# Dealing out the first six transfers of a block exchange between SyncE and GpSimd

## The chip, the cores and the metric

The kernel runs on one NeuronCore of a Trainium2 chip. The metric is the device time of one execution in microseconds (us), the median of several runs. Engines are called as in the profile: PE is TensorE (matmuls; PEld its weight loads), DVE is VectorE, ACT is ScalarE, POOL is GpSimd, SP is SyncE, which here only issues DMAs.

## What is computed

The reference adds an attention output to its input. With eight batches of 512 tokens, width 512, and 16 heads of 32:

```
Q, K, V = heads(x @ W.T + b) for Wq, Wk, Wv
cQ, cK  = Q + heads(tokens @ Wq.T + bq), K + heads(tokens @ Wk.T + bk)
attn    = softmax(cQ @ cK.T / sqrt(32))
out     = x + merge(attn @ V)
```

Everything is float32; `tokens` is one conditioning row per batch.

## The kernel before

**Groups and windows.** The work is cut into 32 groups t = 4b + g: batch b and one of four groups g of four heads. The main loop (line 1237) runs over t, and nearly all of its turns are calls of `thirds(t)` (line 1131). The stretch of such a turn is called *window* t here, counted from PE's first matmul of `weighted(t-1)` (line 856, L808), the product of group t-1's exponentials with V. A turn also makes the scores of group t+1, the transposed exponentials of group t, and a quarter of the next batch's projections (matmuls L461, by a scheme of seven half-size products whose sums are made on DVE and POOL). The order on PE, ACT, DVE and POOL is that of the program text (`manual_schedule`, line 235); SP's instructions, all DMA issues, are placed by the recording layer. Every engine takes its own list strictly in order.

**Exponentials that are kept.** Row maxima and row sums need the scores with queries on partitions; the product with V needs the exponentials with keys on partitions. For groups 2 to 28 (`KEPT`, line 71) the exponentials of the first two query chunks are made once, in `denominators` (L693), kept in SBUF (`room`, line 209) and turned. Those of the other two chunks are made a second time in the other orientation (`exponentials_of_rest`, L766, L777, L787). The turning has two steps: DVE turns 32x32 blocks in place (`turn_kept`, L660), and then six pairs of 32-partition blocks (a, g), a < g, change places by DMA.

**An exchange.** That second step is `swap_kept(t, move)` (line 665), called an *exchange*. It has three rounds of six DMAs of 128 KB each:

- move 0, the *first round*: block (a, g) is copied to a place aside (`between`)
- move 1, the second round: block (g, a) is copied to (a, g), once that one was copied aside
- move 2, the third round: the copy aside goes to (g, a)

SP issues the first three transfers (n = 0, 1, 2) of the first round and all of the second; POOL issues the other three of the first round (n = 3, 4, 5) and all of the third. The first two rounds of exchange t+1 stand at the end of window t (lines 1184 to 1186); the third round stands in the middle of window t+1 (lines 1155 to 1162), ahead of `split_max` on POOL. PE reads the exchanged blocks in the second half of L808 in `weighted(t+1)`, that is in window t+2.

**POOL's list around the first round.** In every window POOL has, in this order: two sums of the output of the group before (`send`, L881 and L882, which wait for DVE's L880), two or three sums of the projection scheme (L535 to L537 for q and k, L1220 and L1221 for v), the third round (six L674), `split_max` (L707 to L710), `masked` (L833), the residual's bias (L204), further sums of the projections (L1209 or L535 to L537), and then POOL's part of the first round of the next exchange (L674). Where t is a multiple of four (a new batch is prepared), `combine_x` (line 380) adds four sums of x for the next batch's projections: L387 and L388 after L204, and L390 and L391 at the end of the window, directly ahead of the first round of exchange t+1. So the exchanges with t % 4 = 1 follow these sums.

**SP's list.** It holds, per window: four loads of the residual (L191), the first and second round, four stores of a finished group (L885), four loads of x (L173), and one transposing DMA of the row maxima (`turn_max`, L719), which waits for `split_max`.

**What waits for POOL's sums.** In window t with t % 4 = 1 the sums L535 to L537 go into DVE's L551 and L486 (`other_products`, lines 551 to 556), which read two PSUM banks. PE needs these banks again for the second pair of the next scores, L641 (`row_max`).

Of the kernel before, what the change touches and what calls it, by code (L numbers as in the profile page):

```python
# [17 lines left out]
def kernel(  # L18
# [38 lines left out]
    nc = tc.nc  # L57
# [606 lines left out]

    def swap_kept(t, move, last=nc.gpsimd):

        def part(a, g):
            return kept[t][a * BL : (a + 1) * BL, g].rearrange("p c h s -> p (c h s)")

        for n, (a, g) in enumerate(APART):  # L670
            at = (n + 2) % HG * BL
            aside = between[at : at + BL, n // HG].rearrange("p i s -> p (i s)")
            to, of = [(aside, part(a, g)), (part(a, g), part(g, a)), (part(g, a), aside)][move]
            (last if move == 2 or move == 0 and n >= 3 else nc.sync).dma_start(to, of)  # L674

    def denominators(t, qc, w=HG, js=range(HG)):

# [453 lines left out]
    def thirds(t, made):  # L1131
# [16 lines left out]
        for i in (1, 2):  # L1148
# [6 lines left out]
            if i == 1:  # L1155
                if t + 1 in KEPT:
                    swap_kept(t, 2)
                split_max(t + 1)
                if t + 1 in KEPT:
                    turn_max(t + 1)  # L1160
                else:
                    swap_kept(t, 2)
# [17 lines left out]
            if i == 2:  # L1180
                if r == 0:
                    combine_x(b + 1, 1, nc.gpsimd)
                load_residual(t + 1)
                if t + 1 in KEPT:
                    for move in range(2):
                        swap_kept(t + 1, move)
            else:
                bias_residual(t)
                if r == 0:
                    combine_x(b + 1, 0, nc.gpsimd)  # L1190
# [104 lines left out]
    def latest_pair(of, among):  # L1295
        pairs = [(j, j + 1) for j in of if j + 1 in of and among & {j, j + 1}]
        return max(pairs, key=lambda p: order.index(p[0]) + order.index(p[1]))

    last = latest_pair(order, {order[7]})
# [59 lines left out]
    t = T - 3  # L1359
# [20 lines left out]
    t = T - 2  # L1380
# [27 lines left out]
    t = T - 1  # L1408
# [103 lines left out]
```

## Time and profile before

| | |
|---|---|
| median of 3 runs | 666.72 us (666.71 to 668.23) |
| the profiled execution | 667.76 us |
| its span, first to last instruction | 666.0 us |
| granted TensorE clock, mean | 0.996 |
| busy PE / DVE / ACT / POOL | 98% / 89% / 81% / 64% of the span |
| DMAs of L674 | 243 issued by SP, 243 by POOL |

The span is one profiled execution; 1.76 us of its time lie outside the span. A busy PE holds waits between matmuls too, since the ends of matmuls are modelled; so it is better to compare how long equal stretches of work take than to read its busy share. In a timeline row stand the start in us, the time taken in us, the engine, the line, the operation, the tiles, the number of merged instructions, and in brackets the idle time before them and what ended it. Windows of the same parity do equal work on PE.

### The profile page before, as it was taken

Reading aid. Unit: us, or ns where it says so; the run is one execution under the profiler, and the core shown is the slowest. Engines: PE = TensorE matmul, PEld = TensorE weight load, DVE = VectorE, ACT = ScalarE, POOL = GpSimd, SP = SyncE. Lnnn points to the kernel's source line nnn. Section 1 sums busy time; section 2 is a strip of 40 time slices with the busy share of each in tenths; the row PEclk is TensorE's granted clock in tenths of the full one; section 3 lists DMA queues with packets and bytes.
Section 4 is the critical chain, followed back from the end, with each engine's and each line's share of the span. In section 5 each row is a group of like instructions: output and inputs, shape, how many; then the busy total and the mean of one; then the engine's idle time right before and its main releaser. Section 6 shows DMA issues by size and latency. Waiting matters only on the chain.

```text
span 666.0 us, 24768 instructions
## 1 busy us (share of the span) xinstructions
PE 652.7 (98%) x9812; PEld 349.4 (52%) x9812; DVE 589.9 (89%) x821; ACT 542.0 (81%) x1378; POOL 423.6 (64%) x668
## 2 busy tenths in 40 slices
PE   9999999999999999999999999999999999999993
PEld 7345445555555555555555555555555555555421
DVE  3698899999999999998999999999999989995793
ACT  2479988889888888988888898888889888887771
POOL 3541345787666876659757696667875597576531
PEclk9999999999999999999999999999999999999998
DMA  6633157778777787877897787779877757786111
GB/s 178 105 51 63 31 122 161 163 165 187 173 152 174 161 190 154 189 156 167 171 190 167 169 191 172 160 150 170 196 165 176 169 133 175 149 181 138 18 18 32
DMA packets 246183, 97.14 MB, mean 146 GB/s; under 512 B 228842, under 2 KB 229354, under 8 KB 246068
## 3 DMA queue, kind: packets, MB, share of 16 engines
q1 hardware_dynamic: 232644, 62.65, 49.3%
q0 software_dynamic: 11664, 31.87, 17.3%
q8 instruction: 77, 1.26, 0.9%
q10 hardware_dynamic: 1760, 1.05, 0.5%
q14 instruction: 38, 0.31, 0.1%
HBM read 19.75 MB, written 8.39 MB: 42 GB/s over the span
## 4 chain that ended last, share of the span: by engine, by line
PE 95%; DMA 2%; SPq 1%; DVE 1%; issue 0%; DVEq 0%
PE psum L461 43%; PE psum L641 19%; PE psum L808 15%; PE psum L777 7%; PE psum L792 3%; PE psum L766 3%; PE psum L748 2%; SPq L270 1%; PE psum L404 1%; DMA w_q<-in_L_cond_Wq_dram 1%; PE psum L745 1%; PE psum L1336 1%; PE psum L818 1%; DMA store<-in_x_dram 1%; DMA w_k<-in_L_cond_Wk_dram 0%; PE psum L843 0%
## 5 line engine op out<-in xcount | busy, mean ns | idle before, releaser
L693 ACT ACTIVATE psum<-psum,nmax 128x512 f32<-128x512 f32 x263 | 174.8, 670 | 5.0 <-DVE nmax L589 3.9
L589 DVE TENSOR_REDUCE nmax<-psum 128x1 f32<-128x512 f32 x219 | 140.5, 678 | 22.2 <-PE psum L641 19.6
L693 ACT ACTIVATE store<-psum,nmax 128x512 f32<-128x512 f32 x190 | 130.3, 700 | 33.3 <-DVE nmax L589 23.8
L650 DVE TENSOR_REDUCE nmax<-psum 128x2 f32<-128x1024 f32 x127 | 153.7, 1211 | 1.3 <-PE psum L641 1.3
L674 POOL DMA_DIRECT2D store<-store x243 | 121.7, 504 | 48.1 <-DMA store<-store 36.2
L641 PE MATMUL psum<-kT,qT 32*128 32x512 f32 x1024 | 146.7, 616 | 0.0
L787 ACT ACTIVATE store<-psum 128x512 f32<-128x512 f32 x216 | 111.5, 603 | 22.6 <-PE psum L777 22.6
L660 DVE STREAM_TRANSPOSE store<-store 128x1024 f32<-128x1024 f32 x108 | 129.5, 1217 | 0.0
L808 PE MATMUL psum<-store,v 128*32 128x256 f32 x1728 | 99.3, 381 | 0.0
L808 PEld LDWEIGHTS psum<-store,v 128*32 128x32 f32 x1728 | 53.2, 110 | 54.1 <-ACT wT_q L628 19.7
L641 PEld LDWEIGHTS psum<-kT,qT 32*128 32x128 f32 x1024 | 57.8, 183 | 37.3 <-issue 20.2
L881 POOL TENSOR_TENSOR res<-res,recs 128x512 f32<-128x512 f32 x30 | 31.4, 1047 | 69.0 <-DVE res L880 68.9
L693 ACT ACTIVATION_READ_ACCUMULATOR psum<-psum,nmax 128x1 f32 x263 | 56.3, 214 | 0.0
L777 PE MATMUL psum<-qT,kT 32*128 32x256 f32 x864 | 55.8, 373 | 0.0
L461 PE MATMUL psum<-wc_v,xc 128*32 128x256 f32 x768 | 47.7, 379 | 0.0
L204 POOL TENSOR_TENSOR xr<-xr,bvs 128x512 f32<-128x512 f32 x30 | 38.4, 1279 | 12.2 <-DMA x<-in_x_dram 11.4
L461 PE MATMUL psum<-xc,wc_k 128*32 128x256 f32 x720 | 44.5, 379 | 0.0
L461 PE MATMUL psum<-xc,wc_q 128*32 128x256 f32 x720 | 44.5, 379 | 0.0
L777 PEld LDWEIGHTS psum<-qT,kT 32*128 32x128 f32 x864 | 42.3, 184 | 3.4
L693 ACT ACTIVATION_READ_ACCUMULATOR store<-psum,nmax 128x1 f32 x190 | 40.8, 215 | 0.0
L882 POOL TENSOR_TENSOR res<-res,xr 128x512 f32<-128x512 f32 x30 | 38.4, 1279 | 2.4
L758 ACT ACTIVATE store<-psum 128x512 f32<-128x512 f32 x56 | 28.9, 603 | 9.3 <-PE psum L748 7.2
(198 smaller groups left out, 1046.3 us busy)
## 6 DMA issues: line engine op xcount, KB each, us to landing
store<-store SPq DMA_DIRECT2D x243, 128.0 KB, 2.8
store<-store POOLq DMA_DIRECT2D x243, 128.0 KB, 3.7
out_dram<-res SPq DMA_DIRECT2D x122, 64.0 KB, 3.6
xr<-in_x_dram SPq DMA_DIRECT2D x120, 64.0 KB, 3.4
x<-in_x_dram SPq DMA_DIRECT2D x112, 64.0 KB, 3.0
w_q<-in_L_cond_Wq_dram SPq DMA_DIRECT2D x4, 256.0 KB, 5.3
w_v<-in_L_cond_Wv_dram SPq DMA_DIRECT2D x16, 64.0 KB, 2.5
w_k<-in_L_cond_Wk_dram SPq DMA_DIRECT2D x16, 48.0 KB, 3.0
```

Source lines behind the costliest of these rows:

```text
L204: nc.gpsimd.tensor_tensor(xr[t], xr[t], bias, ALU.add)
L461: nc.tensor.matmul(pt[r], still[:, r], moving, start=(kc == kcs[0]), stop=(kc == kcs[-1]))
L589: nc.vector.tensor_reduce(nmax[t][:, qc, j : j + 1, 0], pt, AX.X, ALU.max, negate=True)
L641: nc.tensor.matmul(pt, qkT["q", t][r, qc * P : (qc + 1) * P], qkT["k", t][r, :], start=True, stop=True,)
L650: nc.vector.tensor_reduce(nmax[t][:, qc, pr * 2 : pr * 2 + 2, 0], pt, AX.X, ALU.max, negate=True)
L660: nc.vector.transpose(e, e)
L674: (last if move == 2 or move == 0 and n >= 3 else nc.sync).dma_start(to, of)
L693: nc.scalar.activation(to, of, AF.Exp, bias=nmax[t][:, qc, j, :], accum_out=sums[t][:, qc, j, :],)
L777: nc.tensor.matmul(bank[j][:, i * HS : (i + 1) * HS], qkT["k", t][r, kc * P : (kc + 1) * P], qkT["q", t][r, rest], start=False, stop=(i == 1),
L787: nc.scalar.activation(e[:, i, :], bank[pr * 2 + i], AF.Exp)
L808: nc.tensor.matmul(pt[j * HD : (j + 1) * HD, half * HS : (half + 1) * HS], vs[b % 2][:, kc, (g * HG + j) * HD : (g * HG + j + 1) * HD], e, ...
L882: nc.gpsimd.tensor_tensor(y, y, xr.pop(t), ALU.add)
```

## The change

Of an exchange's first round, SP issues the first transfer and POOL the other five, where it was three and three. In exchanges with t % 4 = 1 SP issues all six and POOL none. The second and third rounds stay as they were. For the 27 exchanges (t = 2 to 28) this makes 21 of the first kind and 6 of the second (5, 9, 13, 17, 21, 25).

```diff
     def swap_kept(t, move, last=nc.gpsimd):
 
+        later = 6 if t % 4 == 1 else 1
+
         def part(a, g):
             return kept[t][a * BL : (a + 1) * BL, g].rearrange("p c h s -> p (c h s)")
 
         for n, (a, g) in enumerate(APART):
...
             to, of = [(aside, part(a, g)), (part(a, g), part(g, a)), (part(g, a), aside)][move]
-            (last if move == 2 or move == 0 and n >= 3 else nc.sync).dma_start(to, of)
+            (last if move == 2 or move == 0 and n >= later else nc.sync).dma_start(to, of)
```

The lists of PE, DVE and ACT are the same in both kernels. On POOL the run of three L674 at the end of a window becomes one of five, or goes. On SP the run of nine L674 becomes one of seven, or of twelve.

## The prediction

> **What bounds the kernel now.** I read the page first: PE is busy nearly all the time.
>
> ```profile
> span 666.0 us, 24768 instructions
> PE   652.7 (98%) x9812; PEld 349.4 (52%) x9812; DVE 589.9 (89%) x821; ACT 542.0 (81%) x1378; POOL 423.6 (64%) x668
> ```
>
> The change leaves PE's work alone, so only time in which PE waits can be won. Since a busy PE hides waits, I cut the main loop into windows, each from PE's first L808 to the next, and took their lengths with the stage view of PE alone. Of the 21 windows that are not in the next table, these are the first two, the last, and the sum:
>
> ```profile
> 110.91:130.08 19.17, 19.17 (x316) 1.00 0.76 169
> 130.08:149.45 19.37, 19.37 (x316) 1.00 0.76 169
> ...
> 575.58:594.75 19.17, 19.17 (x316) 1.00 0.74 163
> sum 405.03, PE 405.03; mean PE 19.29
> ```
>
> Column two is the length in us, then come PE's busy time, the clock and the DMA share. Windows with odd t take 19.15 to 19.18, with even t 19.37 to 19.39, and the sum says the same: 10 x 19.165 + 11 x 19.38 = 404.8. Four windows fall out. Here is one that keeps the time (t = 9, the first row) and the four (t = 13, 17, 21, 25), with the busy time of L641 alone:
>
> ```profile
> 226.55:245.70 19.15, 4.18 (x32) 1.79 (x32) 1.00 0.83 179
> 303.63:323.22 19.59, 4.62 (x33) 2.07 (x32) 1.00 0.78 171
> 381.14:400.78 19.64, 4.67 (x33) 1.87 (x32) 1.00 0.81 177
> 458.69:478.52 19.83, 4.86 (x33) 2.06 (x32) 1.00 0.92 176
> 536.45:556.20 19.75, 4.78 (x33) 2.09 (x32) 1.00 0.71 159
> ```
>
> Against the first row they are 0.44, 0.49, 0.68 and 0.60 us longer, **2.21 us** in all, and L641 is longer by the same 0.44, 0.49, 0.68 and 0.60. So PE loses its time at one place, ahead of the second pair of L641. All four are windows with t % 4 = 1, those in which POOL has just made the last sums of x. The timelines of POOL, of window 9 and then of 13:
>
> ```profile
> 230.77 1.52 POOL L674 DMA_DIRECT2D store<-store  x3
> 232.30 1.06 POOL L881 TENSOR_TENSOR res<-res,recs 128x512 f32<-128x512 f32 x1
> 236.17 0.73 POOL L537 TENSOR_TENSOR qT<-qT 128x256 f32<-128x256 f32 x1
> ```
>
> ```profile
> 308.07 1.30 POOL L391 TENSOR_TENSOR xc<-xT,xc 128x512 f32<-128x512 f32 x1
> 309.29 1.52 POOL L674 DMA_DIRECT2D store<-store  x3
> 310.82 1.06 POOL L881 TENSOR_TENSOR res<-res,recs 128x512 f32<-128x512 f32 x1
> 314.70 0.73 POOL L537 TENSOR_TENSOR qT<-qT 128x256 f32<-128x256 f32 x1
> ```
>
> and of DVE, window 9 and then 13, with the weight load that waits in 13:
>
> ```profile
> 237.64 0.41 DVE L551 TENSOR_TENSOR qT<-psum,qT 128x256 f32<-128x256 f32 x1
> 237.97 1.40 DVE L486 SCALAR_TENSOR_TENSOR qT<-psum,tok,qT 128x512 f32<-128x512 f32 x2
> ```
>
> ```profile
> 308.30 0.65 DVE L880 STREAM_TRANSPOSE res<-psum 128x512 f32<-128x512 f32 x1
> 314.77 0.42 DVE L551 TENSOR_TENSOR qT<-psum,qT 128x256 f32<-128x256 f32 x1
> 315.46 1.41 DVE L486 SCALAR_TENSOR_TENSOR qT<-psum,tok,qT 128x512 f32<-128x512 f32 x2 [0.27 <-POOL qT L537]
> ```
>
> ```profile
> 316.93 0.29 PEld L641 LDWEIGHTS psum<-kT,qT 32*128 32x128 f32 x2 [0.20 <-DVE qT L486]
> ```
>
> In window 13 POOL goes from L391 through three DMA issues into L881 without a pause; L537 ends at 315.43; DVE's L486 waits for it, and PE's L641 for L486, whose reads set its banks free. Counted from the window's start, L486 begins at 315.46 - 303.63 = 11.83 us in window 13 and at 237.97 - 226.55 = 11.42 in window 9. That 0.41 is the 0.44 that PE loses. In window 9 L537 ended at 236.90, 10.35 us into the window, 1.07 before L486 began.
>
> **The change part by part.**
>
> *Exchanges with t % 4 = 1 (six of them).* POOL loses three issues between L391 and L881. They take 1.52 us. What is late next? L881 also needs DVE's L880, which ended at 308.95 in window 13, and L391 ended at 309.37; so POOL, not DVE, sets L881, which starts 310.82 - 309.37 = 1.45 us sooner. L537 then ends 315.43 - 1.45 = 313.98, 10.35 us into the window, as in window 9, and L486 finds it done 1.07 us before its time. The worst of the four is window 21:
>
> ```profile
> 470.00 0.73 POOL L537 TENSOR_TENSOR qT<-qT 128x256 f32<-128x256 f32 x1
> ```
>
> It ends at 470.73, or 12.04 into the window, and would end at 10.59: still 0.83 us early. So all four losses go: **-2.2 us** (2.21 against window 9, 2.17 against the 19.16 of its kind). In windows 5 and 9 nothing waits, so there is nothing to win.
>
> SP gets three issues more there. An issue on SP takes 0.54 us in the middle, so twelve take 6.5 us; the nine of before took 8.24:
>
> ```profile
> L674 SPq DMA_DIRECT2D store<-store x243: 507/541/2282, 91.4 to 604.7; - x122
> L674 POOL DMA_DIRECT2D store<-store x243: 489/489/677, 92.4 to 609.5; - x122
> ```
>
> ```profile
> 307.64 8.24 SPq L674 DMA_DIRECT2D store<-store  x9
> ```
>
> since the second round waited for POOL's late copies. That wait goes, so the stores (L885), the x loads and the transposing DMA behind on SP come at about their old times; I take 0, between -1.7 (8.24 to 6.5) and +1.6 (three issues with no wait saved). Their cover is SP's place off the path: no row of PE above waits for it.
>
> *The other 21 exchanges.* POOL gets two issues more, 0.98 us at 489 ns, ahead of L881; 42 x 0.49 = 20.5 us of POOL's time, less 18 x 0.49 = 8.8 in the six. What hides it is POOL's wait there:
>
> ```profile
> POOL res L881 <- DVE res L880: 68.9, 24, 5.0
> POOL store L674 <- DMA store<-store: 36.2, 29, 2.6
> ```
>
> 24 waits with 2.9 us in the mean. The shortest that I found where three issues came in a row is that of window 14:
>
> ```profile
> 328.64 1.04 POOL L881 TENSOR_TENSOR res<-res,recs 128x512 f32<-128x512 f32 x1 [1.24 <-DVE res L880]
> ```
>
> 1.24 holds 0.98. One other is shorter, in window 16, where POOL's third issue came 2.04 us late:
>
> ```profile
> 365.90 0.49 POOL L674 DMA_DIRECT2D store<-store  x1 [2.04 <-issue]
> 367.18 1.04 POOL L881 TENSOR_TENSOR res<-res,recs 128x512 f32<-128x512 f32 x1 [0.78 <-DVE res L880]
> ```
>
> There L881 could come 0.2 us late, for which I count nothing. Cost 0; without the cover at most 0.98 in a window.
>
> SP loses two issues there (1.1 us), but gains little: its second round begins when the first copy has landed, and that one stays on SP behind the residual's loads.
>
> *The shift d.* What the trace can't show is whether the second round, and with it the third on POOL, now ends later by some d in these 21. Two copies come by way of POOL's queue instead of SP's:
>
> ```profile
> store<-store SPq DMA_DIRECT2D x243, 128.0 KB, 2.8
> store<-store POOLq DMA_DIRECT2D x243, 128.0 KB, 3.7
> ```
>
> ```profile
> DMA to landing us min/median/max: 2.2/3.5/6.1
> ```
>
> So d lies between -1.1 (two SP issues saved) and 6.1 - 2.8 = 3.3 (every copy as slow as the slowest). The medians are 0.9 apart, but the second round runs at one issue in 0.54 us from its start, while POOL issues a first-round copy every 0.49, so copies keep ahead of it. I take d = 0, nearest to the medians, and keep both ends. A d matters in window 13 and its like: POOL's third round in windows 12, 16, 20, 24 runs on into L387 to L391 of the next window, so L537 there is later by d. The stall is then max(0, s + d - 1.45), with s = 0.44, 0.49, 0.68, 0.60. Up to d = 0.77 nothing returns; at 0.9 it is 0.13.
>
> The Trainium skill (SBUF — State Buffer, section "A bandwidth-pool intuition that's wrong (but worth ruling out)") speaks against moving issues to GpSimd: a DMA whose descriptors GpSimd writes, some 620 ns alone, takes some 3100 when VectorE holds their common port in a copy. By that rule, as an estimate, five issues would take up to 15 us instead of 2.5, which is rival 3 below with a d of several us. The row of POOL's L674 above disagrees: the longest of 243 issues took 0.677 us, with DVE busy for 89% of the span.
>
> *Sum.* -2.2 + 0 + 0. Span 666.0 to 663.8; the profiled execution 667.76 to 665.6; that one is 1.04 above the median of 666.72, so the median becomes **664.5 us**.
>
> **The rivals.**
>
> 1. *Part of it comes back.* d between 0.8 and 1.45. At d = 1.2 the four stalls are 0.19, 0.24, 0.43 and 0.35, 1.2 in all: 665.7. For it: POOL's third rounds already wait 36.2 us for landings. Against: the first copy, which starts the second round, does not move.
>
> 2. *Nothing measurable.* L641's wait has another cause that ends at the same time, or d is close to 1.45 to 2: 666.7, between 666 and 667.5. For L486 the trace names POOL's L537, and in window 9 POOL is earlier and PE has no wait; that speaks against another cause.
>
> 3. *Slower.* d passes 1.45 and POOL's lag is larger than before. It decides from there: at d = 3 the four stalls are 1.99, 2.04, 2.23 and 2.15, 8.4 us where 2.2 were, and windows 5 and 9 (s = -1.07) get 0.5 each: +7.2, 673.9. PE's read of the exchanged blocks would tell at about the same d. In a tight exchange, 14:
>
> ```profile
> 336.63 2.48 POOL L674 DMA_DIRECT2D store<-store  x5 [2.20 <-DMA store<-store]
> ```
>
> ```profile
> 342.53 2.80 PE L808 MATMUL psum<-store,v 128*32 128x256 f32 x48
> ```
>
> the last copy's issue begins at 338.62 and the read 1.8 us into L808, at 344.3: 5.7 us later, against landings of 3.7 in the middle and 6.1 at most. What speaks against it is the 0.9 between the medians.
>
> **How the numbers follow.** Forecast 664.5 (664.0 to 665.0): 0.64. Rival 1 (665.0 to 666.2): 0.16. Rival 2 (666.2 to 667.5): 0.09. Rival 3 (668 to 676): 0.11. The range 664.0 to 666.5 takes the first two and a little of rival 2, 0.82. A measurement of this kernel can tell about 0.3%, 2.0 us, from no change, and 2.2 lies just over it: below 664.7 I put 0.46, nearly three quarters of the forecast's chance. Slower by over 0.3% is rival 3 and a little of rival 2, 0.12. The rest, 0.42, is within.
>
> **What would show it.** In the changed kernel's trace the windows 13, 17, 21 and 25 should be 19.15 to 19.2 us long with L641 at 4.2; L881 there should follow L391 at once, and L486 have no wait for L537. The other windows should keep 19.16 and 19.38, with L881 still waiting for L880. SP's twelve issues in window 13 should end by about 316. The prediction is wrong if the third round in windows 12, 16, 20, 24 ends more than 0.8 us later in its window than before, if L881 gets late in one of the 21, or if PE's second half of L808 waits for a landing.

## The result, and the profile after

| | before | after |
|---|---|---|
| median of 9 runs | 666.71 us (665.47 to 668.23) | **661.34 us** (659.82 to 668.35) |
| ratio of the times | | **0.9945** (95%: 0.9919 to 0.9971) |
| the profiled execution | 667.76 us | 665.04 us |

The change gains 5.4 us where 2.2 were forecast: faster, by more than the range allowed. The page of after:

```profile
span 662.8 us, 24720 instructions
PE 651.4 (98%) x9812; PEld 350.7 (53%) x9812; DVE 590.1 (89%) x821; ACT 542.7 (82%) x1378; POOL 435.6 (66%) x692
store<-store POOLq DMA_DIRECT2D x267, 128.0 KB, 3.7
```

POOL issues 267 DMAs instead of 243 and PE does the same work. To see where the time went, I cut each span in three with the stage view of PE: the start, the windows t = 3 to 28 (from PE's first L808, L810 in after, of one to that of the next), and the tail behind the start of window 29. The second and the third, of before and of after (columns as in the prediction):

```profile
110.84:614.56 503.72, 503.72 (x8123) 1.00 0.78 169
614.56:665.97 51.41, 39.96 (x400) 0.94 0.12 22
```

```profile
110.08:616.78 506.70, 502.96 (x8123) 1.00 0.79 168
616.78:662.80 46.02, 39.97 (x400) 0.99 0.13 24
```

The windows, where the prediction saw the whole effect, are 3.0 us *longer* in this execution of after. The **tail is 5.39 us shorter**, and in it PE does the same 39.96 us of work. So the gain comes from a stretch in which the change touches no instruction. The clock column of the tails (0.94 and 0.99) does not explain it: the granted clock is 1.00 from 614.56 to 660.0 in before and from 616.78 to 661.7 in after, and 0.50 from 660.2 and from 661.9 on, where PE has no work left (its last matmul ends at 655.6 and 657.8).

What ends the tail? The instructions of the last line (L1507, L1509 in after) that are no arithmetic, before and then after; the columns are the durations in ns (min/median/max) and the first and last start in us:

```profile
L1507 POOLq DRAIN  x3: 34/102/11361, 653.8 to 665.7; - x3
L1507 SPq DRAIN  x3: 7/7/7, 659.3 to 665.5; - x3
```

```profile
L1509 POOLq DRAIN  x3: 34/102/3434, 656.1 to 662.5; - x3
L1509 SPq DRAIN  x3: 7/7/130, 661.6 to 662.3; - x3
```

and POOL's last sum, before and after:

```profile
653.88 1.28 POOL L1432 TENSOR_TENSOR res<-res,store 128x512 f32<-128x512 f32 x1
```

```profile
656.11 1.27 POOL L1434 TENSOR_TENSOR res<-res,store 128x512 f32<-128x512 f32 x1
```

In before POOL's first DRAIN, in which it waits at the end of its list, takes 11.36 us, to 665.2; that is 10.05 after the last sum ended (its end is 655.15 with the decimals of the trace), and SP, which had waited for its last stores, was done at 659.3. POOL sets the end, alone, for 5.8 us. In after the DRAIN ends 2.13 us after the last sum, at 659.5, and SP's wait at 661.6 comes last. The chain of waits of before doesn't show this DRAIN at all; its line by engine is

```profile
PE 95%; DMA 2%; SPq 1%; DVE 1%; issue 0%; DVEq 0%
```

Now the windows of after. The first row is window 13, the others are 18, 21 and 24:

```profile
302.81:321.98 19.17, 19.17 (x316) 1.00 0.80 168
...
399.10:419.85 20.75, 19.49 (x316) 1.00 0.76 170
...
459.04:479.54 20.50, 19.86 (x315) 1.00 0.84 176
...
518.81:539.18 20.37, 19.49 (x316) 1.00 0.82 181
```

Windows 13, 17 and 25 are clean, as forecast (19.17, 19.19 and 19.16). But windows 18 and 20 to 24 lose time at the second half of L810, which reads the exchanged blocks. In window 18, POOL and then PE:

```profile
399.52 0.49 POOL L676 DMA_DIRECT2D store<-store  x1 [2.63 <-issue]
```

```profile
402.29 1.93 PE L810 MATMUL psum<-store,v 128*32 128x256 f32 x32 [1.26 <-DMA x<-in_x_dram]
```

The last copy of exchange 17's third round is issued at 399.52 and lands at 401.99, and PE goes on at 402.29. The brackets do not name what was waited for, but the semaphore instructions in the trace do. PE's, for this copy, lasts from 399.90 to 402.03. POOL's, ahead of the issue at 399.52, lasts from 396.38 to 399.02, until a copy that SP issued at 393.49 has landed (398.99). So a late exchange holds up PE: this is the second place of the prediction's rival 3.

In window 21 the first place is back too. L641 is 4.67 us long there (4.20 in window 13), and POOL and DVE show why:

```profile
471.08 0.73 POOL L537 TENSOR_TENSOR qT<-qT 128x256 f32<-128x256 f32 x1
```

```profile
471.84 1.41 DVE L486 SCALAR_TENSOR_TENSOR qT<-psum,tok,qT 128x512 f32<-128x512 f32 x2 [0.26 <-POOL qT L537]
```

L537 ends 12.77 us into the window, later than before's 12.04, though no issue stands between L391 and L883 any more.

### The profile page after: what moved, and what is told of

Same layout as the page of the kernel before. It is cut to its first block, busy times and chain, and to the rows that moved or that the text cites. A ratio compares the mean times of both kernels' runs of the same rounds, so it can differ in the third digit from the quotient of the medians.

```text
span 662.8 us, 24720 instructions
## 1 busy us (share of the span) xinstructions
PE 651.4 (98%) x9812; PEld 350.7 (53%) x9812; DVE 590.1 (89%) x821; ACT 542.7 (82%) x1378; POOL 435.6 (66%) x692
## 4 chain that ended last, share of the span: by engine, by line
PE 88%; SPq 4%; DMA 4%; DVE 2%; POOL 1%; issue 1%; ACT 0%; DVEq 0%; POOLq 0%
PE psum L461 40%; PE psum L641 17%; PE psum L810 13%; PE psum L779 7%; PE psum L794 3%; PE psum L768 2%; PE psum L404 2%; SPq L676 2%; PE psum L750 2%; SPq L887 2%; DMA store<-store 1%; DMA x<-in_x_dram 1%; DMA out_dram<-res 1%; PE psum L747 1%; PE psum L1338 1%
## 5 line engine op out<-in xcount | busy, mean ns | idle before, releaser
L676 POOL DMA_DIRECT2D store<-store x267 | 133.1, 503 | 55.3 <-DMA store<-store 40.5
L589 DVE TENSOR_REDUCE nmax<-psum 128x1 f32<-128x512 f32 x219 | 140.7, 679 | 25.6 <-PE psum L641 23.2
L641 PE MATMUL psum<-kT,qT 32*128 32x512 f32 x1024 | 144.5, 615 | 0.0
L810 PE MATMUL psum<-store,v 128*32 128x256 f32 x1728 | 100.5, 381 | 3.7 <-DMA x<-in_x_dram 1.4
L810 PEld LDWEIGHTS psum<-store,v 128*32 128x32 f32 x1728 | 53.5, 110 | 58.8 <-ACT wT_q L628 19.7
L641 PEld LDWEIGHTS psum<-kT,qT 32*128 32x128 f32 x1024 | 56.5, 183 | 36.6 <-issue 21.1
L883 POOL TENSOR_TENSOR res<-res,recs 128x512 f32<-128x512 f32 x30 | 31.5, 1051 | 44.0 <-DVE res L882 43.9
```

Of the source, the lines that this page charges most:

```text
L589: nc.vector.tensor_reduce(nmax[t][:, qc, j : j + 1, 0], pt, AX.X, ALU.max, negate=True)
L641: nc.tensor.matmul(pt, qkT["q", t][r, qc * P : (qc + 1) * P], qkT["k", t][r, :], start=True, stop=True,)
L676: (last if move == 2 or move == 0 and n >= later else nc.sync).dma_start(to, of)
L810: nc.tensor.matmul(pt[j * HD : (j + 1) * HD, half * HS : (half + 1) * HS], vs[b % 2][:, kc, (g * HG + j) * HD : (g * HG + j + 1) * HD], e, ...
```

## The experiments

**Theory.** POOL's DRAIN at the end works off something for each DMA that POOL issued, and the change moves where that count stands; the windows give little. **Rivals of this theory.** (1) The gain is in the windows or the exchanges themselves, and the end only follows. (2) The DRAIN goes by bytes or by the rows moved, not by DMAs. (3) All DMAs count, so that more of them make the end later. A mark in the trace helps: ahead of certain issues POOL has a gap that no work before it explains, and through which no semaphore instruction of POOL lasts. In before it is the row 365.90 of the prediction, 2.04 "<-issue". Counting nine issues an exchange, 14 exchanges (t = 2 to 15) make 126, so that issue, the third of exchange 16, is the **129th**. In after exchanges 2 to 14 make 128 (eleven each, six where t % 4 = 1), and again the 129th has a gap, and the 250th too:

```profile
344.62 2.49 POOL L676 DMA_DIRECT2D store<-store  x5 [3.29 <-DVE nmax L589]
...
582.79 0.49 POOL L676 DMA_DIRECT2D store<-store  x1 [2.73 <-issue]
```

(The first is put down to DVE's L589, for which no other of the 267 issues waits.) A mark "<-issue" alone isn't enough: such gaps of over 2 us stand ahead of a few other issues (after's 156th, which is the row 399.52 above, e5's 76th, four in e9), but there a semaphore instruction of POOL lasts nearly as long, so they are waits. The two issues are 121 apart. If the count starts anew with such an issue, 115 stand at the end of before (243 - 128) and 18 at the end of after (267 - 249).

All runs in one table. n is the number of POOL's DMAs from the last such issue on; DRAIN is its end after POOL's last sum, in us; windows and tail are the stretches above; "by the tail" is the tail less before's 51.41; the last two columns compare the medians, of runs on the same chip. In e8 the DRAIN is counted from POOL's own last sum, at 634.93.

| run | POOL's DMAs, n | DRAIN | windows | tail | by the tail | median - before's | ratio (95%) |
|---|---|---|---|---|---|---|---|
| before | 243, 115 | 10.05 | 503.72 | 51.41 | | | |
| after | 267, 18 | 2.13 | 506.70 | 46.02 | -5.39 | 661.34 - 666.71 | 0.9945 (0.9919 to 0.9971) |
| e1 | 267, 18 | 2.13 | 502.01 | 46.00 | -5.41 | 661.18 - 665.21 | 0.9940 (0.9919 to 0.9961) |
| e13 | 267, 18 | 2.13 | 501.76 | 46.01 | -5.40 | 661.52 - 666.20 | 0.9944 (0.9916 to 0.9972) |
| e2 | 225, 97 | 8.58 | 501.64 | 49.95 | -1.46 | 664.38 - 665.21 | 0.9986 (0.9967 to 1.0004) |
| e3 | 285, 36 | 3.60 | 501.62 | 45.19 | -6.22 | 658.59 - 665.21 | 0.9906 (0.9881 to 0.9931) |
| e12 | 285, 36 | 3.60 | 503.01 | 45.20 | -6.21 | 658.72 - 666.20 | 0.9889 (0.9869 to 0.9909) |
| e4 | 267, 18 | 2.13 | 501.64 | 46.05 | -5.36 | 659.90 - 665.21 | 0.9919 (0.9898 to 0.9939) |
| e10 | 267, 18 | 2.13 | 502.44 | 46.02 | -5.39 | 660.13 - 665.45 | 0.9905 (0.9873 to 0.9936) |
| e5 | 243, 115 | 10.05 | 502.58 | 51.42 | 0.01 | 665.22 (one run) | |
| e6 | 249, 121 | 10.54 | 501.68 | 51.91 | 0.50 | 665.44 - 665.14 | 1.0003 (0.9994 to 1.0012) |
| e7 | 250, 1 | 0.74 | 502.01 | 45.58 | -5.83 | 660.11 - 665.14 | 0.9920 (0.9900 to 0.9941) |
| e8 | 243, 115 | 10.05 | 501.80 | 46.38 | -5.03 | 659.92 - 665.14 | 0.9916 (0.9902 to 0.9931) |
| e9 | 162, 34 | 3.44 | 505.61 | 45.51 | -5.90 | 665.58 - 665.45 | 0.9987 (0.9958 to 1.0017) |
| e14 | 297, 48 | 4.58 | 509.15 | 45.94 | -5.47 | 665.40 - 666.20 | 0.9978 (0.9956 to 1.0001) |
| e11 | 0, 0 | 0.07 | 553.81 | 45.81 | -5.60 | 715.49 - 665.45 | 1.0739 (1.0703 to 1.0776) |

From e7 and e6, (10.54 - 0.74) / (121 - 1) = 0.0817 us a DMA, so the DRAIN takes 0.66 + 0.0817 n. Each of the other rows with n over 0 comes out by it within 0.01: 97 gives 8.58, 36 gives 3.60, 18 gives 2.13, 34 gives 3.44, 48 gives 4.58, 115 gives 10.05.

**e1_again and e13_after_third: the change again.** No edit.

> The changed kernel a second time. What is to be told apart: in the first profile of it POOL's last DRAIN ended 2.1 us after POOL's last sum, in that of before 10.0 us after it, and windows 17 to 23 were longer by some 4 us in all than in before. Count theory (POOL pauses at its 129th and 250th DMA issue, and the DRAIN at the end takes about 0.08 us for each DMA issued since the last pause): the DRAIN is again about 2 us after the last sum, and idle stretches of 2 to 3.3 us without a releaser stand ahead of issues 129 and 250. Chance theory (DRAIN and pauses fall anywhere): other lengths and other places. If the long windows 17 to 23 come from the pause at issue 129 they return; if not, the span is about 657.5. Median 660.5 to 662 by both.

> The changed kernel a third time, beside e12: 660.5 to 662 if every fourth exchange costs time by SP's twelve issues; about 659 if not. Its DRAIN is 2.1 us after POOL's last sum by the count theory.

The DRAIN and the tail repeat to 0.02 us. The windows do not: 506.70, 502.01 and 501.76. So the long windows of the first profile of after belong to that execution.

**e2_none_only and e3_five_only: the two parts of the change.**

```diff
-        later = 6 if t % 4 == 1 else 1
+        later = 6 if t % 4 == 1 else 3    # e2_none_only
+        later = 3 if t % 4 == 1 else 1    # e3_five_only, e12_five_again
```

> Only the exchanges with t % 4 = 1 are changed (SP issues all six there; the others stay three and three): POOL issues 225 DMAs. All theories: windows 13, 17, 21, 25 at 19.15 to 19.2, 2.2 us won. Count theory: 225 - 129 = 96 DMAs since the pause, DRAIN about 8.5 us after POOL's last sum, some 4.3 us beyond SP's own end instead of 5.9: 2.2 + 1.6 = 3.8 us won, about 662.9. Chance theory: the same DRAIN as before, 664.5. If the whole gain of 5.4 us belonged to these windows: 661.3.

> Only the other 21 exchanges are changed (POOL issues five; those with t % 4 = 1 stay three and three): POOL issues 285 DMAs. All theories: windows 13, 17, 21, 25 stay longer than 19.2. Count theory: 285 - 250 = 35 DMAs since the second pause, DRAIN about 3.6 us after POOL's last sum, which SP's own end covers: 5.9 us won there, 660.8, less what the pauses cost in the windows. Chance theory or windows alone: 666.7 (0 won).

> Only the other 21 exchanges changed (e3) once more, beside e13 and e14 on one chip. If the part that gives SP all six transfers in every fourth exchange costs time by itself: again 658 to 659.5 and below e13 by 1 us or more. If the 2.6 us between e3 and e1 were scatter: within 0.7 us of e13.

The part on which the whole forecast rested, no issues of POOL where t % 4 = 1, changes the time by -0.8 us alone (the interval holds 1), and the tail alone gives -1.5. The 662.9 expected of e2 had the windows' 2.2 us in it; its median is 664.38. The other part, which was costed at 0, brings 6.6 and 7.5, of which the tail gives 6.2; the rest is within what the windows of one kernel differ by (e3 501.62, e12 503.01). The windows of e3, all like those of e2 though the four were expected to stay long, are no shorter for it (the second and third stretch, of e2 and then of e3):

```profile
109.28:610.92 501.64, 501.64 (x8123) 1.00 0.80 170
610.92:660.87 49.95, 39.97 (x400) 0.95 0.12 22
```

```profile
110.01:611.63 501.62, 501.62 (x8123) 1.00 0.80 170
611.63:656.82 45.19, 39.97 (x400) 0.98 0.13 25
```

Five-only is faster than the whole change by 2.6 us on one chip and by 2.8 on another. Its medians are the lowest of all runs; its ratio to before can't be told from those of e4, e7, e8 and e10, whose values lie in e3's interval. In e3 the 129th is the third issue of exchange 14 and the 250th the seventh of exchange 25, again by counting, and there the gaps are:

```profile
326.11 1.45 POOL L676 DMA_DIRECT2D store<-store  x3 [2.04 <-issue]
...
547.64 1.50 POOL L676 DMA_DIRECT2D store<-store  x3 [2.09 <-issue]
```

**e4_late24, e6_late6, e7_late7, e10_late24_wide: before, with more DMAs of POOL near the end.** The exchanges stay as in before. Behind POOL's `send_parts(t - 1, den)` near the end, where POOL then idles over 10 us, come copies into tiles that nothing reads any more (`free`; the lines left out name these tiles).

```diff
     send_parts(t - 1, den)
...
+    for n in range(24):     # e4_late24; 6 in e6_late6, 7 in e7_late7
+        at = slice(n % 4 * BL, n % 4 * BL + BL)
+        nc.gpsimd.dma_start(free[n // 4 % 3][at], still[at, :1024])
+    # e10_late24_wide instead: free[:, n * 32 : (n + 1) * 32] from still[:, :32]
```

> The kernel before, with 24 more DMAs of 128 KB issued by POOL in the 14 us in which it is idle at the end (copies into tiles that nothing reads any more), so 267 in all as in the changed kernel; the exchanges are untouched. Count theory: the pause of issue 250 falls into that idle time, the DRAIN is about 2 us after POOL's last sum instead of 10, and 5.9 us are won: 660.8, with windows 13, 17, 21, 25 as long as before. Chance theory or windows alone: 666.7, or slower by what the DMAs disturb.

> The kernel before with 6 late DMAs on POOL instead of 24, so 249 in all, one short of the second pause. Count theory: 120 DMAs since the pause at 129, DRAIN 0.74 + 120 x 0.0817 = 10.5 us after POOL's last sum: as slow as before or 0.5 us slower, 665 to 666. If late DMAs of any number shorten the DRAIN: 660.

> One late DMA more than e6: 250 in all. Count theory: the pause of issue 250 falls into POOL's idle time, no DMA is left, DRAIN 0.7 us after POOL's last sum, and the end is set by SP's last stores: 5.8 us faster than before, 659.5 to 660. If the DRAIN goes down smoothly with the count of late DMAs: halfway or less, 664 to 665.

> The kernel before with 24 late DMAs on POOL as in e4, but of 128 rows of 128 bytes instead of 32 rows of 4 KB: more rows, an eighth of the bytes. If pause and DRAIN go by the number of DMAs: 17 since the pause at 250, DRAIN 2.1 us after the last sum, 660. If by bytes: the 24 count as 3, no second pause, DRAIN about 10.3 us, 665. If by rows: the 24 count as 96, the pause comes at the second of them and 88 or so count after it, DRAIN about 8 us, 663.

This separates the theory from its rival (1): with the exchanges untouched, 24 useless DMAs gain 5.3 us, as much as the change. Six gain nothing, seven gain 5.0. POOL's DRAIN in e6, and then in e7, with its late copies:

```profile
L1514 POOLq DRAIN  x3: 34/102/11851, 650.4 to 662.8; - x3
```

```profile
L1514 POOLq DRAIN  x3: 34/102/2049, 650.6 to 656.7; - x3
```

```profile
635.14 3.45 POOL L1402 DMA_DIRECT2D xc<-v  x7
649.54 1.04 POOL L1438 TENSOR_TENSOR res<-res,recs 128x512 f32<-128x512 f32 x1 [10.94 <-DVE res L1436]
```

The seven issues follow one another without a gap, and 10.94 us before the next sum is waited for. One more DMA than in e6, the 250th, shortens the DRAIN by 9.80 us. That rules out rival (3). e10 moves 16 KB a copy on 128 partitions instead of 128 KB on 32, and has the same DRAIN as e4; that rules out rival (2).

**e8_dve_end: the DRAIN as long as in before, but earlier.** The last two sums go to DVE, so that POOL's list ends 20 us sooner.

```diff
-    nc.gpsimd.tensor_tensor(y30, y30, rec.broadcast_to([P, NB, BL]), ALU.mult)
-    nc.gpsimd.tensor_tensor(y30, y30, x30, ALU.add)
+    nc.vector.tensor_tensor(y30, y30, rec.broadcast_to([P, NB, BL]), ALU.mult)
+    nc.vector.tensor_tensor(y30, y30, x30, ALU.add)
```

> The kernel before with its last two sums (L1431, L1432) on DVE instead of POOL; POOL's last sum is then L882, which ended at 638.4 in before. Cover theory (the DRAIN takes its 10 us from POOL's last work on, and only counts where it outlasts the others): it ends near 648.5, beside other work, and nothing of it is left at the end: 5.8 us won, less 0.8 to 1.3 that two sums of 0.65 us cost DVE ahead of L1448: 660 to 661. If the DRAIN waits for the other engines: 665 to 667.

```profile
L1507 POOLq DRAIN  x3: 34/102/11356, 633.6 to 657.2; - x3
```

It takes the same 11.36 us and starts at 633.6, beside PE's last work, and the time falls by 5.2 us with before's exchanges and before's 243 DMAs. So it is the DRAIN's place behind the last sum that costs, not the number of DMAs as such.

**e5_before_again: before once more.** No edit.

> The kernel before a second time, for its windows. In the profile of e4, whose exchanges are those of before, windows 13, 17, 21, 25 took 19.16 to 19.18, without the losses on which the prediction was built. Fixed-loss theory (POOL's order makes the loss): they are 19.6 to 19.8 again. Chance theory (POOL's third rounds end early or late from one execution to the next): other windows, other lengths, or none. Both: the last DRAIN ends about 10.05 us after POOL's last sum, as 114 DMAs were issued since the pause at the 129th.

Windows 13, 17, 21 and 25 of e5, where the prediction had found 2.21 us lost in before:

```profile
302.21:322.27 20.06, 20.06 (x316) 1.00 0.80 174
379.12:398.30 19.18, 19.18 (x316) 1.00 0.72 162
457.31:476.48 19.17, 19.17 (x314) 1.00 0.71 160
534.42:553.59 19.17, 19.17 (x316) 1.00 0.76 160
```

Only window 13 is long. In e4, whose windows have before's instructions, none is (19.16 to 19.18); in e10, with the same instructions, only window 25 is (20.00). Why window 13 is clean in e4, POOL says:

```profile
292.12 2.48 POOL L674 DMA_DIRECT2D store<-store  x5
296.15 0.49 POOL L674 DMA_DIRECT2D store<-store  x1 [1.54 <-DMA store<-store]
...
304.37 1.29 POOL L391 TENSOR_TENSOR xc<-xT,xc 128x512 f32<-128x512 f32 x1
305.60 1.52 POOL L674 DMA_DIRECT2D store<-store  x3
307.67 1.05 POOL L881 TENSOR_TENSOR res<-res,recs 128x512 f32<-128x512 f32 x1 [0.55 <-DVE res L880]
```

and in before:

```profile
294.94 0.55 POOL L674 DMA_DIRECT2D store<-store  x1 [1.39 <-DMA store<-store]
296.79 0.98 POOL L674 DMA_DIRECT2D store<-store  x2 [1.29 <-DMA store<-store]
298.87 1.49 POOL L674 DMA_DIRECT2D store<-store  x3 [1.10 <-DMA store<-store]
```

In before the third round of exchange 12 waited three times for a landing, 3.8 us in all; in e4 once, 1.5. The windows start at 302.18 (e4) and 303.56 by the timeline. So in e4 L391 starts 2.19 us into the window and in before 4.51 (its row 308.07), and the three issues fit ahead of the end of DVE's L880. The loss needs a late third round, and that comes and goes.

**e9_all6, e14_five_always and e11_all_sp: other shares.** All six of the first round on SP; five on POOL always; all eighteen on SP. The edits of e9 and e11 are against before, that of e14 against after.

```diff
-            (last if move == 2 or move == 0 and n >= 3 else nc.sync).dma_start(to, of)
+            (last if move == 2 or move == 0 and n >= 6 else nc.sync).dma_start(to, of)    # e9_all6
+            nc.sync.dma_start(to, of)                                                     # e11_all_sp
-        later = 6 if t % 4 == 1 else 1
+        later = 1                                                                         # e14_five_always
```

> SP issues the whole first round in every exchange; POOL issues only the third rounds, 162 DMAs in all. Count theory: 162 - 129 = 33 DMAs since the pause, DRAIN 0.74 + 33 x 0.0817 = 3.4 us after POOL's last sum, covered by SP's end 4.1 us after it: 5.8 us won, 659 to 660, if SP's twelve issues per exchange do not make the exchanges late. If the split of the first round were worth something by itself, the windows would get longer than 19.16 and 19.38 and the time would be above 661.

> POOL issues five transfers of the first round in all 27 exchanges, so SP never has twelve: 297 DMAs on POOL, 47 since the pause at 250, DRAIN 0.74 + 47 x 0.0817 = 4.6 us after POOL's last sum, 0.4 us or so beyond SP's end. If SP's twelve issues are what costs in the changed kernel: 659 to 659.7, faster than e13. If POOL's issues between L391 and L881 cost in windows 13, 17, 21, 25: slower than e12 by more than the 0.4.

> SP issues all 18 transfers of each exchange, POOL none. Count theory: no pause at a 129th issue and a DRAIN of 0.7 us or less after POOL's last sum; 5.8 us won at the end. Against it SP's list: 18 issues of 0.54 us and 13 others of about as much, some 17 us of 19.3 in a window, and the third round's waits for landings now hold up stores, loads and the transposing DMA behind it: windows longer by 0 to 2 us each, 659 to 700.

All three win over 5 us in the tail, as the theory has it, and miss the 659 to 660 that were expected of e9 and, if the twelve issues on SP were what costs, of e14: they give the gain back in the windows, which are 4.0 (e9), 7.5 (e14) and 52.2 us (e11) longer than the 501.6 of e2 and e3. For e11 up to 700 us was expected; it took 715.5. In e14 the long windows are 13 and 21. Their rows, PE's weight loads waiting as the prediction described it for before, and POOL in window 13:

```profile
302.68:325.92 23.24, 22.58 (x316) 0.93 0.77 160
460.93:483.30 22.37, 20.23 (x315) 1.00 0.79 175
```

```profile
PEld psum L641 <- DVE qT L486: 4.8, 3, 3.0
```

```profile
309.47 2.48 POOL L676 DMA_DIRECT2D store<-store  x5
311.96 1.06 POOL L883 TENSOR_TENSOR res<-res,recs 128x512 f32<-128x512 f32 x1
```

L883 follows the five issues at once. (Not all of the 4 us that window 13 loses is waiting: the granted clock was 0.50 from 318.8 to 322.0.) So issues between L391 and this sum do cost, when there are five of them and POOL comes to them this late. In e11 SP has all eighteen, and PE waits for the copies themselves:

```profile
PE psum L808 <- DMA store<-store: 36.5, 20, 4.0
```

## Why the prediction was wrong

**The step that failed is the sum**, "Span 666.0 to 663.8". It takes the end of the kernel as fixed and moves it by the windows' loss. Before's DRAIN, which stood in its trace and set the last 5.8 us, was no term of it. By the formula the DRAIN falls from 10.05 to 2.13 us, of which 5.8 lay open; SP's wait is late next. The tail measured -5.39, and the medians -5.37, -4.03 and -4.68. Against the tail's gain, each run of after has 2.2 us of its time outside the span where before has 1.8; no run shows why. That the sign of the forecast came out right was luck: the time was won where the sum had no term, and not where it had one.

Could the size have been read from before? Its rows give one DRAIN, 10.05 us behind 243 DMAs; by proportion 267 would make it longer. The sign hangs on the count starting anew at the 250th issue, and before has only 243. What it did show was an open end of 5.8 us on the engine that the change loads, and the row of the 129th issue, which the prediction quoted, with a gap that it left unexplained.

**The four windows, -2.2 us.** The mechanism (L391, the issues, L881, L537, L486, L641) is real: in after L883 waits again for DVE and L537 is early in window 13:

```profile
308.29 1.05 POOL L883 TENSOR_TENSOR res<-res,recs 128x512 f32<-128x512 f32 x1 [3.02 <-DVE res L882]
...
312.14 0.73 POOL L537 TENSOR_TENSOR qT<-qT 128x256 f32<-128x256 f32 x1
```

It ends at 312.87, 10.06 us into the window; the forecast was 10.35. But the 2.21 us were one execution's: e5, the same kernel, has 0.9, and e4, e6, e7, e8 and e10, with the same exchanges, between 0 and 0.8. And taking the issues away doesn't save L537 from a late third round, as window 21 of after showed. e2, which does this part alone, shows no gain beside the tail.

**Two issues more in the other 21, cost 0.** Right for the windows in most executions (e3: 501.62). The DRAIN, which counts those issues, was no term of this cost. **The twelve issues on SP** end early enough (window 13: from 302.99, they take 8.74 us, to 311.7, ahead of the 316 forecast), but not in 6.5 us:

```profile
302.99 8.74 SPq L676 DMA_DIRECT2D store<-store  x12
```

**The shift d, 0.** In the first profile of after it was not: L537 in window 21, forecast to end 10.59 us into the window, ended at 12.77, which makes d 2.2 there, above the 1.45 where the prediction's rival 3 begins. And the late copies of window 18 and on are that rival's second place, PE's read, with window 21 worth 5 us in that execution (506.70 against e13's 501.76). They begin behind the gap at the 129th issue, whose row is above (five issues 3.29 us late at 344.62); that the gap started them is argued, since e1 and e13 have the same gap and lose 0.4 and 0.1 us. In window 18 the copy that POOL waited for took 5.5 us from SP's issue to its landing (393.49 to 398.99), where 2.7 is the median of SP's copies.

**The rule of the Trainium skill** (SBUF — State Buffer, section "A bandwidth-pool intuition that's wrong (but worth ruling out)") would, as the prediction estimates from it, have made POOL's issues several times as long when VectorE copies. In after they are as before, with DVE busy for 89% of the span:

```profile
L676 POOL DMA_DIRECT2D store<-store x267: 492/492/677, 91.6 to 611.7; - x134
```

This says less than the prediction's "disagrees": DVE's full-size copies in this trace read PSUM (L529 and L530, 28 of them, are the largest group), and no run here puts a large copy from SBUF to SBUF on DVE beside these issues.

**Open.** What decides, from one execution to the next, how late a third round is. Why after's median lies 2.6 and 2.8 us above five-only's, where the tail gives 0.8 and the time outside the span 0.4 (2.2 us against 1.8 in each run): the rest must be in the start or the windows, and the profiles of e1 and e13 don't show it (e13's execution, 659.39 us, is the fastest of its twelve). And what the DRAIN does in its 0.08 us a DMA; the runs show only what it counts.

## What to carry to other kernels

Look at the end of the trace before any window: which engine's last instruction ends last, and by how much, because the chain of waits may leave a DRAIN out and a "fixed" end can hang on what was issued hundreds of microseconds before. A loss that is found in one execution is worth checking in a second one before it becomes a term of a sum. And when a small edit moves the time by more than its stretch can hold, cut the span in start, body and tail first: here three rows placed the gain.

## What the runs showed of the hardware

- POOL's DRAIN at the end took 0.66 + 0.0817 us x n, n the DMAs issued by POOL from its 129th or, if it got that far, its 250th on; it goes by DMAs, not by bytes (128 KB and 16 KB alike: 2.13 us).
- Ahead of the 129th issue, in every run that has so many, and of the 250th in after, e1, e3, e12, e13 and e14, POOL stood still 2.0 to 3.3 us, and no semaphore instruction of POOL lasted through it. In e4, e7 and e10, where the 250th is one of the late copies, no gap stands ahead of it, and in e4 and e10 the next issue follows at once too; the count began anew all the same. What makes the gap is open.
- A useless DMA can so be worth 5 us: 249 issues gave 665.44 us, 250 gave 660.11.
